# Three bf16 parts in place of one 32-bit matmul where a graph layer's sums are placed

## The chip, the cores and the metric

The kernel runs on one core of one Trainium2 chip. The metric is the device time of one launch in microseconds (us); the median of three runs of the kernel before is 1866.47 us (1866.22 to 1868.46).

## The reference

One layer of a graph network on 12,500 nodes with 256 channels and 200,000 edges sorted by their target:

```
h    = relu(layernorm(x))                       # 12500 x 256
agg  = segment_sum(h[src], dst, 12500)          # 200000 gathered rows, added by target
z    = (1 + eps) * h + agg
t    = relu(batchnorm(z @ W1 + b1, g1, bt1))    # 256 -> 512, statistics over all nodes
out  = relu(batchnorm(t @ W2 + b2 + h, g2, bt2))
x + out
```

All inputs and outputs are 32-bit floats.

## The kernel before

The kernel has three stages: tables are made ready, then the edges are summed and `z @ W1` is made (up to about 1,670 us of the span), then the second half of the layer follows. The change lies in the middle stage, so only this one is told.

**Groups and steps.** The 1,563 tiles of 128 edges are cut into 131 groups of 12 tiles (`NG`, `GT`). One loop goes over the groups; its pass i is called step i here. Groups 0 to 29 (`LEAD`) are the lead-in: their rows are gathered from `x` and normalised on the way. From group 30 on the rows come from `h_two`, a table in DRAM that holds h times 2048 (`GAIN`) as two 16-bit halves, high and low.

**A regular group** goes through these functions, each in a step of its own, so that several groups are under way at once:

- `gather(i)`: 12 indirect DMAs of 128 rows, issued by POOL (line 649), four regular groups ahead of their use, into one of four buffers.
- `edges(i)`: DVE writes the 0/1 matrix that says which edge belongs to which of 128 target positions (line 712).
- `sums(i)`: PE multiplies it with the gathered rows, 24 16-bit matmuls of 128x256 behind the lead-in (line 753). The sum of a group is 128 positions by 256 channels, in 32-bit floats, in half a bank of PSUM. Behind the lead-in one bank (`ps`) serves all groups: even and odd ones take its two halves in turn.
- `hold(i-1)`, in step i: the finished sum is copied from PSUM to a tile `zs` in SBUF (line 814, DVE behind the lead-in, ACT in it).
- `spots(i-2)`: DVE writes `at`, 128x256, which has one entry per position, at the column where that position lies in a window of 256 nodes. Behind the lead-in the entry is 1/2048 (line 826).
- `put(i-3)`: "placing". For each half of the channels one matmul with `zs` as weights and `at` as moving operand turns the sum and shifts it to its columns; the result is 128 channels by 256 nodes (line 838). A 32-bit matmul stands in the profile as two records, so a put is four.
- `add(i-4)`: DVE adds the placed sum to `zc`, the chunk of 512 nodes that it belongs to (line 856).

When all groups of a chunk are added, `slice_of` multiplies the chunk with a quarter of W1 (line 868, four records), and ACT copies the result out.

**Counted groups.** 22 groups are not gathered. They come in 11 pairs (`COUNTED`: 41 and 42, 50 and 51, up to 122 and 123, then 124 and 125). For a pair the kernel counts how often each node stands among its sources (`count`, line 1073, from marks that DVE writes in lines 1051 and 1058) and multiplies the counts with the whole of `h_two`, read by SP in pieces (`weigh`, line 1091). This work is spread as small units between the matmuls of the regular steps. Its sum is 128x512 for each group of the pair, the high and the low part side by side. `hold_pair` (line 816) adds the two with a `reduce_sum` (line 808) into a place that stays in SBUF, at the step behind the last unit of the pair; that place then goes through `put` as any other. In the steps of the two counted groups themselves PE has only a slice and a put.

**What sets the order.** Each engine works off its own queue in the order in which the program was written; a table (`plan`, `marking`) says which unit falls into which step. In a step behind the lead-in DVE has, in this order: the statistics of the last slice, `add(i-4)`, `edges(i+2)`, `spots(i-2)`, `hold_pair`, `hold(i-1)`, then the marks of this step. PE has, in this order: a slice where one is due, the first two matmuls of `sums(i)`, and then the units and the other matmuls of the group in turn, with `put(i-3)` at about two thirds. The last groups (126 to 130) are handled by `place`, which writes `hold`, `put` and `add` of the same group one right behind the other; groups 129 and 130 go without hold and put.

Of the kernel before, what the change touches and what calls it, by code (L numbers as in the profile page):

```python
# [8 lines left out]
F32 = mybir.dt.float32  # L9
# [9 lines left out]
P = 128  # L19
# [5 lines left out]
LEAD = 30  # L25
# [23 lines left out]
def kernel(  # L49
# [16 lines left out]
    nc = tc.nc  # L66
    N, D = x.shape
# [49 lines left out]
    def move(eng, sb, table, g, store):  # L117
# [33 lines left out]
    lands = [  # L151
        (consts.tile([P, LOW, D], F32, name=f"gta{k}"), consts.tile([P, GT - LOW, D], F32, name=f"gtb{k}"))
        for k in range(EARLY)
    ]
# [29 lines left out]
    at = 0  # L184
# [6 lines left out]
    with ExitStack() as es:  # L191
# [20 lines left out]
        at = 0  # L212
# [9 lines left out]
        with tc.issue_after(placed.ins):  # L222
# [36 lines left out]
            pb, lhsT=first, rhs=dstT[:, : NG * GT].rearrange("p (g t) -> p g t", t=GT)[:, :, 0],  # L259
            start=True, stop=True,  # L260
# [5 lines left out]
        for i in range(EARLY):  # L266
            for t in reversed(range(GT)):
                k = i * GT + t
# [50 lines left out]
        both = raw.tile([1, 12], F32, name="both")  # L319
# [90 lines left out]
    def fast():  # L410

        parts = []
        for n0, w in chunks:
            n = w * R
# [20 lines left out]
        with ExitStack() as fs:  # L435
# [15 lines left out]
            with ExitStack() as es:  # L451
                rows_pool = es.enter_context(tc.tile_pool(name="rows", bufs=RING))
                side_pool = es.enter_context(tc.tile_pool(name="side", bufs=1))
                sel = es.enter_context(tc.tile_pool(name="sel", bufs=2))
# [32 lines left out]
                col, start = near_pe[:, : BLOCKS * WD], near_pe[:, CH - NG :]  # L487
# [185 lines left out]
                def span(i):  # L673
                    return STEP * i - MARGIN, STEP * i - MARGIN + WIDE

                def width(i):
                    return min(WIDE, N - span(i)[0])
# [15 lines left out]
                zc, ohs, summed, zss, ats, placed, slices = {}, {}, {}, {}, {}, {}, {}  # L693
# [110 lines left out]
                def hold(i):  # L804
                    if i in COUNTED:
                        r = COUNTED.index(i) % 2
                        both, zss[i] = totals[r], kept_totals[r]
                        nc.vector.reduce_sum(
                            zss[i], both.rearrange("p (s d) -> p d s", s=2), axis=mybir.AxisListType.X
                        )  # L810
                        return
                    zss[i] = sel.tile([P, D], F32, name="zs", bufs=5)
                    copy = nc.vector.tensor_copy if i >= LEAD else nc.scalar.copy
                    copy(zss[i], summed.pop(i))  # L814

                def hold_pair(i):

                    for j in range(PAIRS_):
                        if i == ended[j] + 1:
                            for k in COUNTED[2 * j : 2 * j + 2]:  # L820
                                hold(k)

                def spots(i):
                    ats[i] = sel.tile([P, WIDE], F32, name="at", bufs=3)
                    n = width(i)
                    nc.vector.tensor_scalar(
                        ats[i][:, :n], col[:, :n], shift[:, i : i + 1], 1.0 if i < LEAD else 1.0 / GAIN,
                        op0=OP.is_equal, op1=OP.mult,
                    )

                def put(i):

                    zs, at = zss.pop(i), ats.pop(i)
                    turn_ = max(i - (NG - CLOSE - 4), 0) % 2
                    pz = own[turn_] if own else ps_z.tile([P, DC, WIDE], F32, name="pz2")
                    n = width(i)
                    for d in range(DC):
                        nc.tensor.matmul(  # L838
                            pz[:, d, :n], lhsT=zs[:, d * P : (d + 1) * P], rhs=at[:, :n], start=True, stop=True
                        )  # L840
                    placed[i] = pz

                def add(i):
# [64 lines left out]
                def half_of(v):  # L908
                    return v.bitcast(BF16)

                def halves_of(tile_, *sizes):

                    v, at, got = tile_.rearrange("p c d -> p (c d)"), 0, []
                    for n in sizes:
                        got.append(v[:, at : at + n // 2])
                        at += n // 2
                    return got

                parts_of, BMARK = [], 0
# [7 lines left out]
                    [v.bitcast(F16).rearrange("p (a m) -> p a m", m=P) for v in of_r[:2]] for of_r in places_  # L927
                ]
                b_places = [of_r[2] for of_r in places_] + halves_of(more[3], *[BMARK] * 7)
                *of_land, total_0, total_1 = halves_of(lands[1][0], *[BMARK] * 4, 2 * D, 2 * D)  # L930
                kept_totals = total_0, total_1
                b_places += halves_of(lands[0][0], *[BMARK] * 4) + of_land
                last_rows, last_a, *more_b = halves_of(spare, ROWS, AMARK, *[BMARK] * 3)
                b_marks = [half_of(v) for v in b_places + more_b]
                a_marks = [
# [9 lines left out]
                totals, keys = [], {}  # L945
# [29 lines left out]
                for j in range(PAIRS_):  # L975
                    until = -(-len(steps) * (j + 1) // PAIRS_)
                    part, done = steps[done:until], until
                    units = [unit for s in range(j * NQ, (j + 1) * NQ) for unit in phase(s)]
                    total, spent = sum(map(price, units)), 0.0
# [8 lines left out]
                for i in sorted(plan):  # L988
                    for kind, s, n in plan[i]:
                        if kind == "count":  # L990
                            j, r = s // NQ, n // WINDOWS
# [109 lines left out]
                def first(c):  # L1101

                    return min(i for i in range(NG) if c in reach(i))
# [18 lines left out]
                for c in range(NCH):  # L1122
                    k = min(max(first(c) - 2, c + 2), NG - CLOSE - 1)
# [4 lines left out]
                for i in range(NG - CLOSE):  # L1128
# [23 lines left out]
                    if i >= 2:  # L1152
                        spots(i - 2)
                    hold_pair(i)
                    while kept <= (i - 2 if kept < LEAD else i - 1):
                        if kept not in COUNTED:
                            hold(kept)
                        kept += 1
# [20 lines left out]
                    def puts():  # L1179
                        if i >= 3:  # L1180
                            put(i - 3)
# [26 lines left out]
                DIRECT, PAIR = NG - 2, (FINAL, FINAL + 1)  # L1208
                assert added == kept - 3 == FINAL - 2 and PAIR == (NG - CLOSE - 2, NG - CLOSE - 1)
                put(FINAL - 1)  # L1210
                spots(NG - CLOSE)
                added_set = set(range(added))
                for c in range(2):
# [3 lines left out]
                def place(k):  # L1217
                    if k < DIRECT:
                        hold(k)
                        put(k)  # L1220
                    place_rest(k)
# [9 lines left out]
                for i in range(NG - CLOSE, NG + 1):  # L1231
# [4 lines left out]
                    if i + 1 < DIRECT:  # L1236
                        spots(i + 1)
# [59 lines left out]
            both = tin.tile([P, 2, CH], F32, name="third")  # L1297
# [27 lines left out]
            with tc.tile_pool(name="ps_y", bufs=2, space=PSUM, reuse_waits="tile") as ps_y:  # L1325
# [165 lines left out]
                p = PAIRS - 1  # L1491
# [309 lines left out]
    with tc.If(off == 0):  # L1801
        fast()
# [32 lines left out]
```

## Time and profile before

| what | value |
|---|---|
| median of three runs | 1866.47 us |
| the profiled execution | 1868.74 us, its span 1866.9 us |
| PE busy | 1604.2 us, 86% of the span |
| DVE busy | 1121.6 us, 60% |
| ACT busy | 827.8 us, 44% |
| POOL busy | 1318.4 us, 71% |
| granted TensorE clock, mean | 0.94 |
| records of line 838 | 428 from `zs`, 88 from kept places: 129 puts of four |
| holds by DVE (line 814) | 77, 423 ns each |

The profile gives for each group of instructions its busy time, the mean of one, and the idle time of the engine just before it with what ended it. The chain of waits is followed back from the last instruction. In the timeline a row is the start, the duration (of all instructions of the row), the engine, the line, the operation, how many, and in brackets the idle time before the first and what ended it. Idle gaps of POOL that say "issue" are time in which POOL waited for nothing that the profile shows.

### The profile page before, as it was taken

The page shows a single profiled execution, that of the slowest core. Times are in us where ns is not written, and L with a number is a line of the kernel's source. Part 1 is how long each engine was busy: PE and PEld are TensorE (multiplying, and loading weights), DVE is VectorE, ACT ScalarE, POOL GpSimd, SP SyncE. Part 2 cuts the span into 40 slices and gives each one's busy share as a digit, 9 for nine tenths or more (in the row PEclk, how much of TensorE's full clock was granted, in tenths as well). Part 3 has the DMA queues.
Part 4 walks back from the last instruction along what each step waited for, and adds up shares of the span by engine and source line. Part 5 has one row for each costly group of instructions (what it writes and reads, how often), then busy time and mean ns, then how long its engine had stood idle before and what let it go on. Part 6 is the DMA issues. An engine that isn't in the chain of part 4 may idle for free.

```text
span 1866.9 us, 22422 instructions
## 1 busy us (share of the span) xinstructions
PE 1604.2 (86%) x7812; PEld 991.4 (53%) x7812; DVE 1121.6 (60%) x1723; ACT 827.8 (44%) x1537; POOL 1318.4 (71%) x1345
## 2 busy tenths in 40 slices
PE   3565676777689999999999999999999999989996
PEld 2454454555455555555555555555555555554445
DVE  6666666674854564646465364756455473448997
ACT  3776676776233333333333333333333333325546
POOL 7777777777777777777777777777777777715640
PEclk9777887888799999999999999999999999999999
DMA  6576676766467887888888788887888888859898
GB/s 199 174 223 215 211 222 211 218 201 195 138 195 246 257 256 242 267 270 253 255 262 265 240 256 270 257 251 246 273 259 263 268 250 277 239 176 324 307 337 320
DMA packets 173063, 456.66 MB, mean 245 GB/s; under 512 B 30883, under 2 KB 58699, under 8 KB 172941
## 3 DMA queue, kind: packets, MB, share of 16 engines
q1 hardware_dynamic: 95657, 258.63, 41.4%
q0 software_dynamic: 62336, 170.28, 31.8%
q10 hardware_dynamic: 14948, 26.23, 3.9%
q8 instruction: 63, 1.03, 0.2%
q14 instruction: 59, 0.48, 0.1%
HBM read 390.97 MB, written 64.05 MB: 244 GB/s over the span
## 4 chain that ended last, share of the span: by engine, by line
PE 57%; DVE 12%; DMA 10%; POOL 10%; issue 6%; ACT 4%; SPq 0%; ACTq 0%; POOLq 0%; DVEq 0%
PE ph L1091 11%; PE ps L1091 10%; PE ps L753 9%; POOL gt L649 8%; PE ph L1073 6%; PE ph L868 5%; DVE stg L520 4%; PE pz L838 4%; PE pz L1073 3%; DMA gta<-in_x_dram,srcT 3%; PE one L1374 3%; DMA gt<-in_x_dram,srcT 2%; PE pr L1374 2%; PE pq L1374 2%; DMA more<-in_x_dram,srcT 2%
## 5 line engine op out<-in xcount | busy, mean ns | idle before, releaser
L649 POOL DMA_INDIRECT gt<-h_two,srcT x939 | 889.9, 948 | 286.3 <-issue 277.2
L753 PE MATMUL ps<-gt,oh 128*128 128x256 f16 (+1 forms) x2136 | 425.1, 296 | 26.7 <-DVE zs L814 23.6
L1078 ACT CAST more<-ph 128x420 f16<-128x420 f32 (+1 forms) x437 | 224.6, 517 | 367.3 <-PE ph L1073 363.4
L856 DVE TENSOR_TENSOR zc<-pz,zc 128x512 f32<-128x512 f32 (+7 forms) x185 | 92.0, 523 | 385.2 <-PE pz L838 385.2
L753 PEld LDWEIGHTS <-oh 128*128 128x128 f16 x1848 | 182.7, 99 | 217.0 <-issue 50.0
L1091 PE MATMUL ph<-gtb,more 128*128 128x512 f16 x720 | 274.3, 381 | 1.2 <-DMA gtb<-h_two 1.2
L1091 PE MATMUL ps<-gtb,more 128*128 128x512 f16 x720 | 272.7, 379 | 0.0
L1091 PEld LDWEIGHTS <-more 128*128 128x128 f16 x2156 | 212.4, 99 | 111.6 <-issue 2.8
L868 PE MATMUL ph<-zc,w1s 128*128 128x512 f32 (+1 forms) x304 | 166.0, 675 | 69.3 <-ACT ts L886 33.4
L1078 ACT CAST more<-pz 128x420 f16<-128x420 f32 (+1 forms) x223 | 115.4, 517 | 165.3 <-PE pz L1073 161.3
L712 DVE TENSOR_TENSOR oh<-col,dstT 128x1536 f16<-128x1536 f32 (+1 forms) x107 | 187.2, 1750 | 0.0
L649 POOL DMA_INDIRECT gt<-in_x_dram,srcT x144 | 140.3, 974 | 43.9 <-issue 18.9
L1051 DVE TENSOR_TENSOR more<-col,keys 128x1536 bf16<-128x1536 f32 x88 | 152.1, 1751 | 0.8
L838 PE MATMUL pz<-at,zs 128*128 128x256 f32 x428 | 120.6, 407 | 28.5 <-DVE zc L856 22.8
L1073 PEld LDWEIGHTS <-more 128*128 128x128 bf16 x1056 | 103.4, 98 | 65.8
L1091 PE MATMUL ph<-oh,more 128*128 128x512 f16 x358 | 136.1, 380 | 0.7 <-DMA oh<-h_two 0.7
L1091 PE MATMUL ps<-oh,more 128*128 128x512 f16 x358 | 135.5, 378 | 0.0
L886 ACT COPY ts<-ph 128x512 f32<-128x512 f32 x74 | 43.4, 586 | 190.8 <-PE ph L868 163.2
L868 PEld LDWEIGHTS ph<-zc,w1s 128*128 128x128 f32 x304 | 60.1, 214 | 119.6 <-issue 58.4
L838 PEld LDWEIGHTS pz<-at,zs 128*128 128x128 f32 x428 | 82.1, 206 | 51.8 <-DVE zc L856 29.9
L649 POOL DMA_INDIRECT gta<-in_x_dram,srcT x80 | 80.8, 1010 | 24.4 <-issue 11.3
L814 DVE COPY zs<-ps 128x256 f32<-128x256 f32 x77 | 32.6, 423 | 107.1 <-PE ps L753 107.1
(265 smaller groups left out, 2487.5 us busy)
## 6 DMA issues: line engine op xcount, KB each, us to landing
gtb<-h_two SPq DMA_DIRECT2D x176, 512.0 KB
oh<-h_two SPq DMA_DIRECT2D x88, 512.0 KB
t_tab<-ts ACTq DMA_DIRECT2D x96, 256.0 KB
gt<-h_two,srcT POOLq DMA_INDIRECT x939, 4.1
h_two<-more SPq DMA_DIRECT2D x24, 512.0 KB
h_cols<-gt SPq DMA_DIRECT2D x24, 512.0 KB
zc<-h_cols SPq DMA_DIRECT2D x24, 512.0 KB
yT<-h_cols SPq DMA_DIRECT2D x24, 512.0 KB
```

What stands on the lines that cost most here:

```text
L520: reader = nc.vector.bn_stats(st[:, c : c + 2, :].rearrange("p c s -> p (c s)"), two.rearrange("p c d -> p d c"),)
L649: fetch = nc.gpsimd.indirect_dma_start(out=slot(ga, t - t0)[:rows], out_offset=None, in_=x if i < LEAD else h_two, in_offset=bass.Indirect ...
L712: nc.vector.tensor_tensor(oh, col[:, :P].unsqueeze(1).to_broadcast([P, n, P]), dstT[:, t0 : t0 + n].unsqueeze(2).to_broadcast([P, n, P]), ...
L753: part = nc.tensor.matmul(ps, lhsT=lhsT, rhs=side, start=(j == order[0] and side is sides[0]), stop=(j == order[-1] and side is sides[-1]),)
L838: nc.tensor.matmul(pz[:, d, :n], lhsT=zs[:, d * P : (d + 1) * P], rhs=at[:, :n], start=True, stop=True)
L856: nc.vector.tensor_add(side, pz[:, :, a - lo : b - lo], side)
L868: nc.tensor.matmul(ph[:, :n], lhsT=w1s[:, d, f * P : (f + 1) * P], rhs=zc[c][:, d, :n], start=(d == 0), stop=(d == DC - 1),)
L1051: nc.vector.tensor_tensor(a_marks[n % len(a_marks)], col[:, :P].unsqueeze(1).to_broadcast([P, GT, P]), keys[r][:, q, :].unsqueeze(2).to_br ...
L1073: nc.tensor.matmul(ph[:, :wide].rearrange("p (a d) -> p a d", d=WD)[:, :, lo:hi], lhsT=a_mark[:, w * WT + t, :], rhs=b_mark[:, at : at + b ...
L1078: nc.scalar.copy(counts[r][s % 2][:, : blocks(q), w * WD : (w + 1) * WD], ph[:, :wide].rearrange("p (a d) -> p a d", d=WD),)
L1091: nc.tensor.matmul(totals[r], lhsT=counts[r][s % 2][:, a % BLOCKS, :], rhs=rows[:, at, :], start=(a == 0), stop=(a == NB - 1),)
L1374: nc.tensor.matmul(ps, lhsT=w[:, k, :], rhs=t[:, k, :], start=(k == 0), stop=(k == DC - 1))
```

## The change

Behind the lead-in `hold` makes three bf16 parts of the 32-bit sum, and `put` takes three 16-bit matmuls for each half of the channels, added up in PSUM:

- ACT rounds the sum to bf16 (part 0). DVE subtracts part 0 from the sum, in place, rounds the remainder (part 1) and subtracts that again, which leaves part 2. For a regular group the sum is worked on where it lies, in its half of the PSUM bank; for a counted one `reduce_sum` now writes a small tile `zc` in SBUF, of which there is one, and the parts go to the kept place, which grows from 512 to 768 16-bit numbers.
- `at` is written as bf16 behind the lead-in; 1/2048 is exact in it.
- the tile `zs` is half as long again, and there are three of it, not five.

In the lead-in the sum is copied by ACT as before, and placed by one 32-bit matmul a half.

```diff
                 def hold(i):
                     if i in COUNTED:
                         r = COUNTED.index(i) % 2
-                        both, zss[i] = totals[r], kept_totals[r]
-                        nc.vector.reduce_sum(
-                            zss[i], both.rearrange("p (s d) -> p d s", s=2), axis=mybir.AxisListType.X
-                        )
+                        zss[i], both = kept_totals[r], totals[r]
+                        z = sel.tile([P, D], F32, name="zc", bufs=1)
+                        nc.vector.reduce_sum(z, both.rearrange("p (s d) -> p d s", s=2), axis=mybir.AxisListType.X)
+                    else:
+                        zss[i], z = sel.tile([P, 3 * D // 2], F32, name="zs", bufs=3), summed.pop(i)
+                    if i < LEAD:
+                        nc.scalar.copy(zss[i][:, :D], z)
                         return
-                    zss[i] = sel.tile([P, D], F32, name="zs", bufs=5)
-                    copy = nc.vector.tensor_copy if i >= LEAD else nc.scalar.copy
-                    copy(zss[i], summed.pop(i))
+                    zss[i] = of_three(zss[i])
+                    nc.scalar.copy(zss[i][:, 0, :], z)
+                    nc.vector.tensor_sub(z, z, zss[i][:, 0, :])
+                    nc.vector.tensor_copy(zss[i][:, 1, :], z)
+                    nc.vector.tensor_sub(zss[i][:, 2, :], z, zss[i][:, 1, :])
+
+                def of_three(v):
+                    return half_of(v).rearrange("p (k d) -> p k d", k=3)
...
                     ats[i] = sel.tile([P, WIDE], F32, name="at", bufs=3)
+                    if i >= LEAD:
+                        ats[i] = half_of(ats[i])
...
+                    parts_ = [zs] if i < LEAD else [zs[:, k, :] for k in range(3)]
                     for d in range(DC):
-                        nc.tensor.matmul(
-                            pz[:, d, :n], lhsT=zs[:, d * P : (d + 1) * P], rhs=at[:, :n], start=True, stop=True
-                        )
+                        for part in parts_:
+                            nc.tensor.matmul(
+                                pz[:, d, :n], lhsT=part[:, d * P : (d + 1) * P], rhs=at[:, :n],
+                                start=part is parts_[0], stop=part is parts_[-1],
+                            )
                     placed[i] = pz
...
-                *of_land, total_0, total_1 = halves_of(lands[1][0], *[BMARK] * 4, 2 * D, 2 * D)
-                kept_totals = total_0, total_1
-                b_places += halves_of(lands[0][0], *[BMARK] * 4) + of_land
+                kept_totals = []
+                for k in range(2):
+                    *of_land, total = halves_of(lands[k][0], *[BMARK] * 4, 3 * D)
+                    b_places += of_land
+                    kept_totals.append(total)
```

`half_of` reads a 32-bit tile as twice as many bf16 numbers. Lines behind the change move: line 838 of before is 850 of the change, 856 is 869, 868 is 881, 1051 and 1058 are 1066 and 1073, 1073 and 1091 are 1088 and 1106.

Three places show how the instructions stand. First DVE's queue at a step with `hold_pair` (here the seventh pair), from the add to the marks. Before:

```order
L856 TENSOR_TENSOR zc<-pz_3136,zc 128x2x256 [waits DVE_49,PE_49]
L712 TENSOR_TENSOR oh<-col,dstT 128x1536
L826 TENSOR_SCALAR at<-col,shift 128x256
L808 TENSOR_REDUCE gta_80<-ph 128x256 [waits PE_49]
L808 TENSOR_REDUCE gta_80<-ps 128x256 [waits PE_49]
L814 COPY zs<-ps 128x256 [waits PE_49]
L1051 TENSOR_TENSOR more_347<-col,keys 128x1536 x2
```

And of the change (`gta_78` and `gta_80` are where the kept sums of the pair lie, `zc` with 256 columns is the small tile, `ps` the bank of the regular sums):

```order
L836 TENSOR_SCALAR at<-col,shift 128x256
L809 TENSOR_REDUCE zc<-ph 128x256 [waits PE_49]
L817 TENSOR_TENSOR zc<-zc,gta_78 128x256 [waits Activation_49]
L818 CAST gta_78<-zc 128x256 [waits DVE_49]
L819 TENSOR_TENSOR gta_78<-zc,gta_78 128x256 [waits DVE_49]
L809 TENSOR_REDUCE zc<-ps 128x256 [waits DVE_49,PE_49]
L817 TENSOR_TENSOR zc<-zc,gta_80 128x256 [waits Activation_49]
L818 CAST gta_80<-zc 128x256 [waits DVE_49]
L819 TENSOR_TENSOR gta_80<-zc,gta_80 128x256 [waits DVE_49]
L817 TENSOR_TENSOR ps<-ps,zs 128x256 [waits Activation_49]
L818 CAST zs<-ps 128x256 [waits DVE_49]
L819 TENSOR_TENSOR zs<-ps,zs 128x256 [waits DVE_49]
```

Where three instructions stood, eleven stand, all ahead of the marks, and three of them wait for ACT. ACT's queue at the same step, of the change (the last counts of the step before stand ahead, the copy of the slice behind):

```order
L1093 CAST more_346<-ph 128x20x21 [waits PE_49]
L816 CAST gta_78<-zc 128x256 [waits DVE_49]
L816 CAST gta_80<-zc 128x256 [waits DVE_49]
L816 CAST zs<-ps 128x256 [waits PE_49]
L899 COPY ts<-ph 128x512 [waits PE_49]
```

Before, ACT had nothing between these two. PE's queue at the same step, where a slice stands ahead of the first matmul of the group. Before:

```order
L868 MATMUL ph<-zc,w1s 128x512 [waits whole5,Activation_49]
L868 MATMUL ph<-zc,w1s 128x512
L753 LDWEIGHTS oh
L753 MATMUL ps<-gt,oh 128x256 [waits DVE_49]
L753 LDWEIGHTS oh
L753 MATMUL ps<-gt,oh 128x256
```

And of the change:

```order
L881 MATMUL ph<-zc,w1s 128x512 [waits whole5,Activation_49]
L881 MATMUL ph<-zc,w1s 128x512
L753 LDWEIGHTS oh
L753 MATMUL ps<-gt,oh 128x256 [waits DVE_49]
L753 LDWEIGHTS oh
L753 MATMUL ps<-gt,oh 128x256
```

The first matmul of a group waits for DVE in both: before for the copy in line 814 of the group ahead, in the change for line 819 of the group ahead, the last of its hold. A put is one row `L838 MATMUL pz_3136<-at,zs 128x256 x2` before, and six pairs of LDWEIGHTS and MATMUL in line 850 in the change.

## The prediction

> **What bounds the kernel now.** I read the page, the waits, the timeline of single steps, the groups by form, and the windows for the clock. The waits first (who waited for whom: us, times, longest):
>
> ```profile
> POOL gt L649 <- issue: 296.1, 971, 0.3
> PE ps L753 <- DVE zs L814: 23.6, 16, 7.8
> PE pz L838 <- DVE zc L856: 22.8, 11, 7.9
> PE ph L868 <- DMA gt<-h_two,srcT: 15.0, 10, 3.0
> ```
>
> No gap of POOL is longer than 0.3 us: the gathers run at their own pace and never wait for a buffer. PE waits ten times for gathered rows, 15.0 us in all. So PE and the gathers are nearly even: whatever makes PE faster is soon lost in waits for rows, and whatever makes PE slower lasts, once those few us are eaten. The gathers end early enough to leave the end to PE:
>
> ```profile
> 1640.64 0.94 POOL L649 DMA_INDIRECT gt<-h_two,srcT  x1 [0.30 <-issue]
> 1653.52 0.78 PEld L798 LDWEIGHTS <-gt 128*128 128x128 f16 x8
> ```
>
> The last gather is issued at 1640.64; PE begins with group 129, the last full one, at 1653.52. The end of this stage is PE's, and in its last steps DVE's. What PE waits for at the start of a step shows here, without a slice and with one:
>
> ```profile
> 1153.39 0.38 PE L753 MATMUL ps<-gt,oh 128*128 128x256 f16 x2
> 1154.29 0.60 PE L753 MATMUL ps<-gt,oh 128*128 128x256 f16 x4 [0.51 <-DVE zs L814]
> ...
> 1165.97 0.38 PE L753 MATMUL ps<-gt,oh 128*128 128x256 f16 x2
> 1166.19 1.88 PE L868 MATMUL ph<-zc,w1s 128*128 128x512 f32 x4
> 1167.91 0.60 PE L753 MATMUL ps<-gt,oh 128*128 128x256 f16 x4
> ```
>
> Without a slice PE's next group starts 0.90 us after the last two matmuls of the one before, held by DVE's hold, although it writes the other half of the bank. With a slice the start is 1.94 us later, and a hold of 0.42 us is hidden. [...]
>
> **What the change saves.** A put and the 16-bit matmuls of the same width, near the end:
>
> ```profile
> 1648.52 1.47 PE L753 MATMUL ps<-gt,oh 128*128 128x256 f16 x12
> 1649.83 1.03 PE L838 MATMUL pz<-at,gta 128*128 128x256 f32 x4
> 1650.70 0.49 PE L753 MATMUL ps<-gt,oh 128*128 128x256 f16 x3
> ```
>
> Twelve take 1.31 us, 0.109 each; a put takes 0.87. Six 16-bit ones are 0.65, so a put saves 0.21 us. 99 puts lie behind the lead-in, 21 us in all.
>
> **What it adds to the hold.** The prices, by form:
>
> ```profile
> L814 DVE COPY zs<-ps 128x256 f32<-128x256 f32 x77 | 32.6, 423 | 107.1 <-PE ps L753 107.1
> L814 ACT COPY zs<-ps 128x256 f32<-128x256 f32 x30 | 11.2, 372 | 33.8 <-PE ps L753 32.6 <-ACT ts L886 1.2
> L856 DVE TENSOR_TENSOR zc<-pz,zc 128x256 f32<-128x256 f32 x16 | 6.0, 417 | 17.5 <-PE pz L838 17.5
> L808 DVE TENSOR_REDUCE gta<-ph 128x256 f32<-128x512 f32 x11 | 7.6, 691 | 18.1 <-PE ph L1091 18.1
> L886 ACT COPY ts<-ph 128x512 f32<-128x512 f32 x74 | 43.4, 586 | 190.8 <-PE ph L868 163.2
> L588 ACT ACTIVATE more<-more 128x1024 f16<-128x1024 f32 x16 | 16.9, 1058 | 0.5
> ```
>
> ```profile
> 1651.51 0.15 DVE L767 TENSOR_TENSOR off<-shift,row 128x1 f32<-128x1 f32 x1
> 1651.69 0.23 DVE L769 TENSOR_SCALAR to<-dstT,off 128x3 f32<-128x3 f32 x1
> ```
>
> Before, one copy of 0.42. Now ACT 0.37, then three instructions of DVE of 0.42, each of which needs the one before; L769, which reads what L767 wrote, started 0.03 behind its end. 0.37 + 0.03 + 3 x 0.45 make 1.75; of the last 0.45 only the instruction's own 0.42 counts, which leaves 1.72. Against the 0.42 of before that is 1.30; Handing on from engine to engine may take a little longer than from DVE to itself, so I take 1.36. Whether ACT's rounding or DVE's writing into PSUM costs more, no row shows: the bounds are 1.05 (the three overlapping, 0.34 apart, as independent copies do) and 1.70 (0.1 more for each). What it does to PE, place by place:
>
> 1. *Steps without a slice*: PE waits for all of it, +1.36. From group 43 to 121 there are 63 regular steps; leaving out the first of each run of seven and the steps with a pair, I count 14 of this kind in the timeline: 19 us.
>
> 2. *Steps with a slice*: the hold now ends 0.90 + 1.36 = 2.26 after the last matmuls, the slice at 1.94: +0.32, in 31 steps: 10 us.
>
> 3. *Steps with hold_pair.* The seventh pair:
>
> ```profile
> 1239.73 0.69 DVE L808 TENSOR_REDUCE gta<-ph 128x256 f32<-128x512 f32 x1 [0.88 <-PE ph L1091]
> 1240.94 0.41 DVE L814 COPY zs<-ps 128x256 f32<-128x256 f32 x1
> 1241.69 0.38 PE L753 MATMUL ps<-gt,oh 128*128 128x256 f16 x2
> ```
>
> The hold that PE waits for stands behind the pair's in DVE's queue. Before, it was through at 1241.35, in time. Now each of the two is 0.69 for the reduce, 0.42 for ACT from SBUF (1058 ns for 1024 columns, less 768 columns at 0.83 ns, the slope from 372 ns for 256 columns to 586 for 512), 0.03 behind both, and three times 0.45: 2.5; two are 5.0, and the group's own three are 1.35. PE starts 6.4 us behind the first reduce, not 1.96: +4.4 us (3.4 to 5.5), ten times before the end: 44 us. Nothing covers it: PE's units of this step stand behind the waiting matmul.
>
> 4. *Steps of counted groups.* There PE's second put waits for the add ahead, and that add stands in DVE's queue behind hold and marks:
>
> ```profile
> 1072.82 0.42 DVE L814 COPY zs<-ps 128x256 f32<-128x256 f32 x1 [1.41 <-PE ps L753]
> 1077.10 0.74 DVE L856 TENSOR_TENSOR zc<-pz,zc 128x256 f32<-128x256 f32 x2
> 1077.90 2.05 PE L838 MATMUL pz<-at,zs 128*128 128x256 f32 x4 [2.53 <-DVE zc L856]
> ```
>
> I find such a wait, 2.53 here, at nine of the ten places, so +1.36 each: 12 us. At the tenth (from 1597) DVE itself waits for the slice, and hides it.
>
> 5. *The tail.* Here hold, put and add of a group follow one another:
>
> ```profile
> 1644.02 1.10 PE L838 MATMUL pz<-at,zs 128*128 128x256 f32 x4 [0.61 <-DVE zs L814]
> 1647.56 1.13 PE L838 MATMUL pz<-at,gta 128*128 128x256 f32 x4 [1.78 <-DVE at L826]
> 1652.76 1.13 PE L838 MATMUL pz<-at,zs 128*128 128x256 f32 x4 [1.24 <-DVE zs L814]
> ```
>
> Groups 126 and 127 +1.36 each, the pair +3.6, group 128 +0.9 (ACT is done early): 7 us.
>
> Sum: 19 + 10 + 44 + 12 + 7 = 92. Off go the puts that lie on the path, some 80 of the 99 (those whose end waits for DVE anyway and those before group 40 do not count): 17. Off go also the waits for rows from group 40 on, about 10 of the 15.0. That leaves +62 us.
>
> **The clock.** In rows of 3.4 us (engines' busy us, then PEclk):
>
> ```profile
> 1040.40:1043.80 3.40, 3.40 (x4) 1.25 (x5) 1.66 (x1) 0.00 (x0) 2.49 (x4) 0.50 0.59 211
> 1282.80:1286.20 3.40, 1.27 (x5) 0.84 (x5) 3.40 (x7) 0.59 (x1) 2.57 (x3) 1.00 0.73 198
> 1286.20:1289.60 3.40, 3.40 (x5) 1.19 (x5) 3.40 (x8) 0.00 (x0) 2.71 (x3) 0.50 0.40 121
> 1392.00:1395.40 3.40, 1.58 (x6) 1.24 (x7) 3.40 (x7) 1.15 (x1) 2.49 (x4) 1.00 0.85 254
> 1395.40:1398.80 3.40, 3.40 (x18) 1.77 (x18) 3.37 (x8) 1.30 (x3) 2.62 (x3) 1.00 0.49 122
> ```
>
> After a stretch in which PE was busy 1.27 of 3.40 us the clock was 0.50 for the next; after 1.58 it stayed at 1.00. So idling over about 2 us within one stretch costs up to 1.7 us. The ten waits of 4.4 us must each do this; a part of the half-speed stretch is still idle, so I take 1.4: 14 us. The nine of point 4 grow by 1.36, this one to 3.9, and do it more often than before: net 4. The drop at 1040 comes from waits for rows; that it goes, I count -2. Net +16. [...]
>
> The sum is 62 + 16 = +78 us, made against the profiled execution's 1868.74 (span 1866.9 and 1.8 around it), which lies 2.3 over the median of the runs. For the median: 1866.5 + 78 = 1944 us.
>
> **The rivals.**
>
> [...]
> - *A longer chain*: 0.1 us more for each instruction (1.70 and 5.5) gives 14 x 1.7 + 31 x 0.66 + 55 + 9 x 1.7 + 9 - 27 = 96, and drops on nearly all waits, 25: 1987 us. No row shows DVE writing back into the bank it reads.
> - *The rows decide*, and DVE's chain is hidden: if the first matmul of a group were not held by the bank, only points 4 and 5 would stay, and less than the waits for rows takes up; a few us in the tail remain, 1869 us. Against it stands 0.51 in the row of 1154.29.
> - *Faster*: all 21 us of the puts come through, 1846 us. It needs the hold to be hidden behind the slice, so a chain less than 1.04 us longer (1.94 less 0.90), and gathers that end sooner; POOL has only its 0.3 us gaps to give. It decides only if PE were the sole bound and DVE never asked.
>
> That three 16-bit matmuls are no cheaper than one of 32 bits is excluded by 0.65 against 0.87.
>
> **How the numbers follow.** The main case has 0.50, no more drops 0.24, the longer chain 0.17, rows decide 0.05, faster 0.04. The likeliest gives 1944. With the short bounds (1.05 and 3.4, no drops) the sum is 14 x 1.05 + 34 + 9 x 1.05 + 5 - 27 = 36, 1902; the long one gives 1987. For 8 in 10 I take nearly all of that, 1905 to 1985. A measurement here can tell about 0.2%, 3.7 us, from no change: faster 0.04, same 0.04 (most of the rows' case), slower 0.92.
>
> **What would show it.** In the profile of the changed kernel: line 753 idle for DVE's line 819, not 23.6 but some 75 us, with ten waits over 4 us; six records of line 850 in 0.65 us; lines 817 to 819 near 420 ns each; POOL with gaps over 0.3 us that PE's line 753 ends; more stretches at half clock. Wrong would be the prediction if those ten waits were absent, or if PE still waited for rows in the second half.

## The result, and the profile after

The changed kernel takes 1968.89 us (median of six runs), the kernel before 1865.67 us beside it: 1.056 times as long, interval 1.0545 to 1.0575. It is 103 us slower; one of the six took 5718 us, a slow run that the ratio and its interval leave out. The forecast was slower by 78, 1944 us in a range of 1905 to 1985: the sign and the range held, and the size was 25 us short. The profiled execution of the change has a span of 1966.2 us, 99.3 more than that of before; the rest of this text divides these 99.3.

The waits of the change (who waited for whom: us, times, longest), where before line 753 waited 23.6 us for DVE and POOL never lost more than 0.3 us at a time:

```profile
POOL gt L649 <- PE ps L753: 94.0, 48, 13.7
PE ps L753 <- DVE zs L819: 92.6, 43, 8.7
PE pz L850 <- DVE zc L869: 38.4, 12, 7.7
PE ph L881 <- DMA gt<-h_two,srcT: 7.8, 4, 2.7
```

PE waits for DVE's last instruction of a hold, and now POOL waits for PE: a gather finds its buffer still in use for 94 us in all. PE's waits for gathered rows at the slice fell from 15.0 to 7.8 us. The gathers, which were even with PE, are now held back by it.

The groups by form give the new instructions (busy us, mean ns):

```profile
L817 DVE TENSOR_TENSOR ps<-ps,zs 128x256 f32<-128x256 f32 x77 | 33.2, 431 | 138.3 <-ACT zs L816 138.3
L818 DVE CAST zs<-ps 128x256 bf16<-128x256 f32 x77 | 32.7, 424 | 2.7
L819 DVE TENSOR_TENSOR zs<-ps,zs 128x256 bf16<-128x256 f32 x77 | 32.6, 424 | 2.6
L816 ACT CAST zs<-ps 128x256 bf16<-128x256 f32 x77 | 28.7, 373 | 45.4 <-PE ps L753 43.5
L818 DVE CAST gta<-zc 128x256 bf16<-128x256 f32 x22 | 6.9, 312 | 0.8
```

Each of DVE's three instructions takes what the one copy took, as priced; writing back into PSUM costs next to nothing (431 against 424 ns), and ACT's rounding takes what its copy took (373 against 372). The one price that is off is the rounding of a counted sum out of SBUF, 312 ns and not 420.

A start without a slice and one with a slice, of the change:

```profile
1190.64 0.38 PE L753 MATMUL ps<-gt,oh 128*128 128x256 f16 x2
1192.87 0.60 PE L753 MATMUL ps<-gt,oh 128*128 128x256 f16 x4 [1.84 <-DVE zs L819]
...
1204.34 0.38 PE L753 MATMUL ps<-gt,oh 128*128 128x256 f16 x2
1204.56 1.88 PE L881 MATMUL ph<-zc,w1s 128*128 128x512 f32 x4
1206.57 0.60 PE L753 MATMUL ps<-gt,oh 128*128 128x256 f16 x4
```

Between the starts of the last matmuls of one group and the first of the next lie 2.23 us in both cases, against 0.90 and 1.94 before: +1.33 and +0.29 (forecast +1.36 and +0.32). Now the step with the seventh hold_pair, DVE first and then PE:

```profile
1282.53 0.69 DVE L809 TENSOR_REDUCE zc<-ph 128x256 f32<-128x512 f32 x1 [0.88 <-PE ph L1106]
1283.69 0.42 DVE L817 TENSOR_TENSOR zc<-zc,gta 128x256 f32<-128x256 f32 x1 [0.47 <-ACT gta L816]
...
1285.04 0.69 DVE L809 TENSOR_REDUCE zc<-ps 128x256 f32<-128x512 f32 x1
1286.21 0.43 DVE L817 TENSOR_TENSOR zc<-zc,gta 128x256 f32<-128x256 f32 x1 [0.47 <-ACT gta L816]
...
1287.36 0.42 DVE L817 TENSOR_TENSOR ps<-ps,zs 128x256 f32<-128x256 f32 x1
1288.28 0.42 DVE L819 TENSOR_TENSOR zs<-ps,zs 128x256 bf16<-128x256 f32 x1
```

```profile
1282.76 1.88 PE L881 MATMUL ph<-zc,w1s 128*128 128x512 f32 x4
1288.76 0.59 PE L753 MATMUL ps<-gt,oh 128*128 128x256 f16 x2 [4.12 <-DVE zs L819]
1289.71 0.64 PE L753 MATMUL ps<-gt,oh 128*128 128x256 f16 x2
```

PE starts 6.2 us behind the first reduce (forecast 6.4, before 1.96). The rows behind the wait show a second part of the price: two matmuls take 0.59 to 0.64 us where they take 0.38 elsewhere. The windows give the clock (the seventh column after the time range):

```profile
1283.70:1287.10 3.40, 0.94 (x3) 0.21 (x2) 2.69 (x7) 1.17 (x3) 2.49 (x4) 0.99 0.95 377
1287.10:1290.50 3.40, 1.74 (x8) 1.02 (x8) 3.33 (x6) 0.51 (x1) 2.48 (x4) 0.50 0.71 193
```

From the starts of all groups in both traces the 99.3 us divide so:

| where | forecast | measured |
|---|---|---|
| steps without a slice (13 places) | 19 | 15.4 |
| steps with a slice (32) | 10 | 9.9 |
| steps with hold_pair (10) | 44 | 37.3 |
| boundaries at counted groups (9) | 12 | 16.7 |
| waits for rows that vanish | -10 | within the rows above |
| shorter puts and slower clock, within the groups 39 to 120 | -17 + 16 | +9.2 |
| tail, from the start of group 121 to the end of the stage | 7 | 7.9 |
| rest: up to group 39 -1.8, last stage +4.7 | 0 | +2.9 |
| sum | 81 | 99.3 |

The first four rows are the growth of the time between the last matmul of a group and the first of the next. Of the rest, the part up to the start of group 30 (-4.3) and the last stage (+4.7) are not touched by the change. Over the eight undisturbed traces here the last stage lies between 202.6 and 207.3 us; before has the shortest and the change the longest, so I take that difference for chance. Groups 30 to 38 cost 2.5.

### The profile page after: what moved, and what is told of

Its sections match the earlier page's. It is cut to its first block, busy times and chain, and to the rows that moved or that the text cites. A ratio compares the mean times of both kernels' runs of the same rounds, so it can differ in the third digit from the quotient of the medians.

```text
span 1966.2 us, 23146 instructions
## 1 busy us (share of the span) xinstructions
PE 1614.6 (82%) x8010; PEld 984.3 (50%) x8010; DVE 1209.0 (61%) x1943; ACT 860.9 (44%) x1636; POOL 1319.0 (67%) x1345
## 4 chain that ended last, share of the span: by engine, by line
PE 52%; DVE 18%; DMA 10%; POOL 6%; ACT 6%; issue 5%; SPq 0%; ACTq 0%; DVEq 0%; POOLq 0%
PE ph L1106 11%; PE ps L1106 10%; PE ps L753 9%; PE ph L1088 6%; POOL gt L649 5%; DVE stg L520 4%; PE pz L1088 3%; PE pz L850 3%; DMA gta<-in_x_dram,srcT 3%; PE one L1389 3%; PE ph L881 2%; DMA gt<-in_x_dram,srcT 2%; PE pr L1389 2%; PE pq L1389 2%; DMA more<-in_x_dram,srcT 2%
## 5 line engine op out<-in xcount | busy, mean ns | idle before, releaser
L753 PE MATMUL ps<-gt,oh 128*128 128x256 f16 (+1 forms) x2136 | 433.2, 300 | 94.6 <-DVE zs L819 92.6
L1106 PE MATMUL ph<-gtb,more 128*128 128x512 f16 x720 | 279.9, 389 | 1.1 <-DMA gtb<-h_two 1.1
L1106 PE MATMUL ps<-gtb,more 128*128 128x512 f16 x720 | 277.6, 386 | 0.0
L850 PE MATMUL pz<-at,zs 128*128 128x256 bf16 (+1 forms) x582 | 105.3, 316 | 45.1 <-DVE zc L869 37.8
L817 DVE TENSOR_TENSOR ps<-ps,zs 128x256 f32<-128x256 f32 x77 | 33.2, 431 | 138.3 <-ACT zs L816 138.3
L1410 POOL TENSOR_TENSOR ax<-ax,by 128x1024 f32<-128x1024 f32 x10 | 27.3, 2726 | 85.6 <-ACT by L1367 81.7
```

What stands on the lines that cost most here:

```text
L753: part = nc.tensor.matmul(ps, lhsT=lhsT, rhs=side, start=(j == order[0] and side is sides[0]), stop=(j == order[-1] and side is sides[-1]),)
L850: nc.tensor.matmul(pz[:, d, :n], lhsT=part[:, d * P : (d + 1) * P], rhs=at[:, :n], start=part is parts_[0], stop=part is parts_[-1],)
L1106: nc.tensor.matmul(totals[r], lhsT=counts[r][s % 2][:, a % BLOCKS, :], rhs=rows[:, at, :], start=(a == 0), stop=(a == NB - 1),)
```

## The experiments

Two sets of runs (those labelled below as the first and second disturbed set) were taken while everything ran slowly: the kernel before itself took 2379 and 2336 us there, and the chip of the first set gave 1865 in another. What slowed it stays open, since these traces lack two thirds of the records that tell of a DMA's landing. POOL was held up in them as it is not before (its longest wait before is 0.3 us), here in the kernel with the puts alone:

```profile
POOL gt L649 <- PE ps L753: 417.8, 69, 21.3
```

In such a set the place of a wait can't be priced, so the argument rests on the runs of other sets.

**The chain alone: only regular groups are split.** Counted groups are summed straight into the kept place as before, and placed by one 32-bit matmul a half.

```diff
                     if i in COUNTED:
                         r = COUNTED.index(i) % 2
-                        zss[i], both = kept_totals[r], totals[r]
-                        z = sel.tile([P, D], F32, name="zc", bufs=1)
-                        nc.vector.reduce_sum(z, both.rearrange("p (s d) -> p d s", s=2), axis=mybir.AxisListType.X)
-                    else:
-                        zss[i], z = sel.tile([P, 3 * D // 2], F32, name="zs", bufs=3), summed.pop(i)
+                        zss[i] = kept_totals[r][:, :D]
+                        nc.vector.reduce_sum(
+                            zss[i], totals[r].rearrange("p (s d) -> p d s", s=2), axis=mybir.AxisListType.X
+                        )
+                        return
+                    zss[i], z = sel.tile([P, 3 * D // 2], F32, name="zs", bufs=3), summed.pop(i)
...
-                    if i >= LEAD:
+                    if i >= LEAD and i not in COUNTED:
                         ats[i] = half_of(ats[i])
...
-                    parts_ = [zs] if i < LEAD else [zs[:, k, :] for k in range(3)]
+                    parts_ = [zs] if i < LEAD or i in COUNTED else [zs[:, k, :] for k in range(3)]
```

> Once more, only regular groups are split in three parts, in PSUM as in the change; counted ones are held and placed as before. My theory: the waits of about 6 us in the steps with hold_pair fall to 2.1 to 2.3, some 36 us in ten steps, with them the half-speed stretches behind them (18 us, as the filled waits showed), and 4 us in the tail, against 4 more for 32-bit puts: about 1915 us (1905 to 1925). Rival, the pair matters little and the chain of every step makes the loss: 1950 or more.

Measured: 1915.1 us, 1.0267 times before (1.0249 to 1.0284), 54 less than the change. The same step, PE:

```profile
1260.66 0.38 PE L753 MATMUL ps<-gt,oh 128*128 128x256 f16 x2
1260.88 1.88 PE L882 MATMUL ph<-zc,w1s 128*128 128x512 f32 x4
1263.25 0.38 PE L753 MATMUL ps<-gt,oh 128*128 128x256 f16 x2 [0.48 <-DVE zs L820]
```

The start is 2.59 us behind the last matmuls, not 6.2. From group 43 on, the nine groups that follow such a wait are 18.7 us shorter together than in the change, and the gaps at their ends are the same. So about half of the loss belongs to the counted pairs (54 us) and half to the regular chain (50). The same kernel in the first and second disturbed set:

> Only regular groups are split in three parts, counted ones are held and placed as before. My theory: the waits of about 6 us in the ten steps with hold_pair fall to 2.1 to 2.3, some 38 us, with them the half-speed stretches behind them, some 17, and 4 us in the tail, against 4 more for 32-bit puts: about 1912 us (1900 to 1922). Rival, the pair matters little and the chain of every step makes the loss: 1950 or more.

> Only regular groups are split in three parts, in PSUM as in the change; counted ones are held and placed as before. My theory: the waits of about 6 us in the steps with hold_pair fall to 2.1 to 2.3, some 36 us in ten steps, with them the half-speed stretches behind them (18 us, as the filled waits showed), and 4 us in the tail, against 4 more for 32-bit puts: about 1915 us (1905 to 1925). Rival, the pair matters little and the chain of every step makes the loss: 1950 or more.

There 2417.6 and 2373.0 us, 1.017 and 1.014 times before. The counterpart, only the counted groups split, was run in these two sets alone:

> Only counted groups are split in three parts, regular ones are held by one copy and placed by one 32-bit matmul a half. My theory: steps without a pair start as before (0.79 and 1.83 us behind the last matmuls), the ten with hold_pair wait about 5.1 us, 32 us more than before, the clock drops behind them cost 16 and the tail 4: about 1912 us (1900 to 1922). Rival, only the regular chain counts: 1870.

> Only counted groups are split in three parts; regular ones are held by one copy and placed by one 32-bit matmul a half. My theory: steps without a pair start as before (0.79 and 1.83 us behind the last matmuls), the ten with hold_pair wait about 5.1 us, 32 us more than before, the clock drops behind them cost 18 and the tail 4, the boundaries little: about 1918 us (1905 to 1928). Rival, only the regular chain counts: 1870.

2402.2 and 2358.4 us, 1.0097 and 1.0094 times before. Both halves cost something there too (none of the four intervals reaches down to 1.005); the sizes expected for an undisturbed chip are not tested by them.

**The order in DVE's queue.** The regular hold stands ahead of the pair's.

```diff
-                    hold_pair(i)
                     while kept <= (i - 2 if kept < LEAD else i - 1):
                         if kept not in COUNTED:
                             hold(kept)
                         kept += 1
+                    hold_pair(i)
```

> Once more, the changed kernel with hold(i-1) ahead of hold_pair in DVE's queue. My theory: the two banks of the pair stay taken for as long, so PE's wait moves from the first matmul of the group to the first weighing of the next pair, about 1.3 us behind it, and is 1 to 2 us shorter: 1955 us (1942 to 1965). Rival, the order in DVE's queue alone makes the wait: it falls to 2.3 us, and time to about 1915.

Measured: 1945.8 us, 23 less than the change, 1.0441 times before (1.0422 to 1.046). The start of the group is at 2.2 us again, and the wait moved, as expected, but not to where I put it:

```profile
1272.78 0.38 PE L753 MATMUL ps<-gt,oh 128*128 128x256 f16 x2
...
1273.51 0.46 PE L1088 MATMUL ph<-more,more 128*128 128x420 bf16 x2
1276.78 0.46 PE L1088 MATMUL ph<-more,more 128*128 128x420 bf16 x2 [2.80 <-ACT ts L899]
```

PE waits 2.8 us at the third count, for the bank that ACT frees by copying the slice out. That copy stands in ACT's queue behind the pair's two roundings, and each of those waits for DVE's reduce (in the seventh pair's step of the change ACT idles 2.59 and 2.12 us before them, until DVE's line 809 ends). So the pair's split holds PE through a third engine's queue, and the order in DVE's queue was worth 23 of the 54 us that the pair costs. In the first disturbed set the same kernel took 2422.4 us, 1.0162 times before:

> The changed kernel with hold(i-1) ahead of hold_pair in DVE's queue. My theory: the two banks of the pair stay taken for as long, so PE's wait moves from the first matmul of the group to the first weighing of the next pair, about 1.3 us behind it, and is 1 to 2 us shorter: 1955 us (1942 to 1965). Rival, the order in DVE's queue alone makes the wait: it falls to 2.3 us, and time to about 1915.

**The clock by itself.** In nine of the ten steps with hold_pair 16 idle matmuls of 512 columns go into the bank of the slice, which the slice then overwrites. The tenth, at the start of group 57, has no slice and stays as it was.

```diff
+                    if fill is not None:
+                        for _ in range(FILL):
+                            nc.tensor.matmul(
+                                ph, lhsT=last_oh[fill][:, 0, :], rhs=last_oh[fill][:, 1:5, :].rearrange("p a b -> p (a b)"),
+                                start=True, stop=True,
+                            )
                     for d in range(DC):
                         nc.tensor.matmul(
                             ph[:, :n], lhsT=w1s[:, d, f * P : (f + 1) * P],
```

> The changed kernel with 16 idle 16-bit matmuls of 512 columns (some 3.5 us) ahead of the slice in the steps with hold_pair, into the bank that the slice then overwrites. PE still waits for the hold, but it is busy while it does. My theory: the wait itself costs the same, and the clock does not drop behind it, 2 us in each of eight or nine steps: about 1951 us (1944 to 1958). Rival, the 2 us that the group behind a pair's step loses have another cause, or idling is not what lowers the clock: 1969, or more where the idle matmuls are in the way.

Measured: 1948.8 us, 20 less than the change, 1.0454 times before (1.042 to 1.0488). The same step (lines are two higher):

```profile
1276.22 0.38 PE L755 MATMUL ps<-gt,oh 128*128 128x256 f16 x2
1276.44 3.62 PE L884 MATMUL ph<-oh 128*128 128x512 f16 x16
1279.89 1.88 PE L889 MATMUL ph<-zc,w1s 128*128 128x512 f32 x4
1282.38 0.38 PE L755 MATMUL ps<-gt,oh 128*128 128x256 f16 x2 [0.60 <-DVE zs L821]
```

The group starts as late as in the change, 6.2 us behind the last matmuls, but PE idles 0.60 us and not 4.12, and its first matmuls take 0.38 us. From group 43 on, eight waits are filled. The groups behind them are 16.9 us shorter than in the change, 1.7 to 2.7 each, with the same gaps at their ends, and none of the eight waits is followed by half speed any more. At group 57, without a fill, PE waits 5.84 us and the clock drops as in the change. More work on PE made the kernel faster: such a wait costs its length and, through the clock, about 2 us more.

**The bank freed at once.** Every sum leaves PSUM with one instruction (a copy, or the reduce) into a 32-bit tile, and the split works on that, behind all copies of the step. DVE has one instruction more for each regular group than in the change. There is one such tile for the regular groups and one for each of a pair; a pool of three tiles for all groups would leave 4.84 KB per partition of SBUF for another pool of 6 KB.

```diff
+                        z = sel.tile([P, D], F32, name="zc", bufs=1)
+                        nc.vector.tensor_copy(z, summed.pop(i))
+                    unsplit.append((zss[i], z))
+
+                unsplit = []
+
+                def split():
+                    while unsplit:
+                        parts, z = unsplit.pop(0)
+                        nc.scalar.copy(parts[:, 0, :], z)
+                        nc.vector.tensor_sub(z, z, parts[:, 0, :])
+                        nc.vector.tensor_copy(parts[:, 1, :], z)
+                        nc.vector.tensor_sub(parts[:, 2, :], z, parts[:, 1, :])
...
                             hold(kept)
                         kept += 1
+                    split()
```

> Every sum leaves PSUM with one instruction (DVE's copy for a regular group, reduce_sum for a counted one, into 32-bit tiles in SBUF, one for each), as before the change; the split into three parts then works on that tile, behind the holds of the step and ahead of the marks. DVE does one copy more for each group than in the changed kernel. My theory (what costs is that the bank stays taken through the split): the starts of groups are as before, 0.79 and 1.83 us behind the last matmuls and about 2 in the ten steps with hold_pair, puts save 17 us, of which waits for rows take some 10 back; the adds of counted steps stay late, some 16, and the tail 8: about 1878 us (1865 to 1892). Rival, DVE's extra work itself is what costs (late marks, late adds): 1950 or more, since DVE has more to do than in the change.

Measured: 1885.4 us, 1.0116 times before (1.0098 to 1.0135), 84 less than the change. The seventh pair's step on DVE:

```profile
1239.28 0.69 DVE L813 TENSOR_REDUCE gta<-ph 128x256 f32<-128x512 f32 x1 [0.88 <-PE ph L1116]
1239.88 0.68 DVE L813 TENSOR_REDUCE gta<-ps 128x256 f32<-128x512 f32 x1
1240.48 0.42 DVE L817 COPY zc<-ps 128x256 f32<-128x256 f32 x1
1240.81 0.42 DVE L826 TENSOR_TENSOR gta<-gta 128x256 f32<-128x256 f32 x1
```

Three instructions end what PE waits for. In 34 of the 54 steps from group 44 to 121 that are no boundary, the next group now starts 0.21 us sooner than before, the price of the shorter put, to the hundredth as forecast; in most of the others one of the two traces has a wait for a DMA or a stretch at half speed. What stays are the nine boundaries, 19 us together, and the tail, since there the add, or the put, stands behind the split. It was how long the bank is held, and not DVE's load: DVE has more to do here than in the change, a copy of 0.42 us for each regular group. The run moves two things at once, the work on the bank and the order (no split stands ahead of a copy any more); the order alone was worth 23 us above.

**The split behind the add.** In the first step of a counted pair the split follows the next step's add.

```diff
                             hold(kept)
                         kept += 1
-                    split()
+                    if not (i in COUNTED and i + 1 in COUNTED):
+                        split()
...
                         added = take_and_add(added)
+                        if i in COUNTED:
+                            split()
```

> As the run in which sums are copied out of PSUM first, but in the first step of a counted pair the split stands behind the next step's add, not ahead of the marks. My theory: the nine boundaries at counted pairs, 2.1 us each over before, go back to what they were (19 us), and the rest stays: 1885 - 19 = 1866 us (1859 to 1875). Rival, the boundaries are late for another reason (DVE has 1.3 us more to do in each step): 1883.

Measured: 1885.4 us, 1.0107 times before (1.0087 to 1.0127): nothing gained, 19 us off. The mechanism worked and the time did not follow. The nine boundaries fell by 23 us; but the other steps of groups 43 to 121 grew by 16.5, with more waits for gathered rows, and the tail by 4.6:

```profile
PE ph L890 <- DMA gt<-h_two,srcT: 17.2, 7, 3.8
PE ps L753 <- DMA gt<-h_two,srcT: 7.4, 4, 3.0
```

In the run with the copy these two were 9.3 and 3.0 us. I had carried the rows as a term once and left them out here.

**The tail as before, too.** Groups from 124 on are held and placed as before the change; all others as in the last run.

```diff
+                    if i >= FINAL:
+                        if i in COUNTED:
+                            r = COUNTED.index(i) % 2
+                            zss[i] = kept_totals[r][:, :D]
+                            nc.vector.reduce_sum(
+                                zss[i], totals[r].rearrange("p (s d) -> p d s", s=2), axis=mybir.AxisListType.X
+                            )
+                            return
+                        zss[i] = sel.tile([P, 3 * D // 2], F32, name="zs", bufs=3)
+                        nc.vector.tensor_copy(zss[i][:, :D], summed.pop(i))
+                        return
...
-                    if i >= LEAD:
+                    if LEAD <= i < FINAL:
                         ats[i] = half_of(ats[i])
...
-                    parts_ = [zs] if i < LEAD else [zs[:, k, :] for k in range(3)]
+                    parts_ = [zs] if i < LEAD or i >= FINAL else [zs[:, k, :] for k in range(3)]
```

> As the run with the split behind the add, and groups from 124 on (the last pair and 126 to 128) are held and placed as before the change, by one copy and one 32-bit matmul a half. My theory: the tail, some 9 us over before in the run with the copy, comes back: 1857 us (1850 to 1865), below the kernel before, since some 80 puts are 0.21 us shorter and nothing waits for the split any more; waits for rows may take half of it. Rival, the rows decide and nothing is gained over before: 1866.

Measured: 1870.0 us, 1.003 times before (1.0019 to 1.0041). The tail came back, and the rival was nearer than my theory: nothing is gained over before. The first and the last gather from `h_two`, of before and then of this run, and this run's waits for rows:

```profile
465.67 0.95 POOL L649 DMA_INDIRECT gt<-h_two,srcT  x1 [0.30 <-ACT more L547]
1640.64 0.94 POOL L649 DMA_INDIRECT gt<-h_two,srcT  x1 [0.30 <-issue]
```

```profile
462.27 0.95 POOL L649 DMA_INDIRECT gt<-h_two,srcT  x1 [0.30 <-ACT more L547]
1642.70 0.95 POOL L649 DMA_INDIRECT gt<-h_two,srcT  x1 [0.30 <-issue]
```

```profile
PE ph L901 <- DMA gt<-h_two,srcT: 22.4, 10, 4.1
PE ps L753 <- DMA gt<-h_two,srcT: 5.9, 4, 2.7
```

The 939 gathers start 3.4 us sooner and end 2.1 later than before. However much sooner PE is ready, it waits for rows: 22.4 us at the slice against 15.0 before, and 5.9 at line 753 against 3.1. That is how I read where the gain of the shorter puts went; no run has faster gathers, so it is not shown by an experiment. Why a gather takes 1.258 us on average here and 1.253 before is open.

**The puts alone** were tried only in the first disturbed set.

```diff
-                    nc.scalar.copy(zss[i][:, 0, :], z)
-                    nc.vector.tensor_sub(z, z, zss[i][:, 0, :])
-                    nc.vector.tensor_copy(zss[i][:, 1, :], z)
-                    nc.vector.tensor_sub(zss[i][:, 2, :], z, zss[i][:, 1, :])
+                    nc.vector.tensor_copy(zss[i][:, 0, :], summed.pop(i))
...
-                    parts_ = [zs] if i < LEAD else [zs[:, k, :] for k in range(3)]
+                    parts_ = [zs] if i < LEAD or i in COUNTED else [zs[:, 0, :] for k in range(3)]
```

> The placing alone is changed: a regular sum is copied once by DVE, as bf16, and that one part is placed three times (so parts 1 and 2 are left out, and the result is not the reference's); counted groups stay wholly as before. My theory: a put of six records 0.65 us against 0.87, 77 puts, 16 us of PE's time off, some of it lost in waits for rows: 1855 us (1850 to 1862). Rival, the new form of put is itself no cheaper where it stands: 1866.

2389.1 us, 1.0045 times before (1.0018 to 1.0072): no gain, which rows that decide would give too, but no test of 1855 us on an undisturbed chip.

## Why the prediction was right, and where it was short

**What bounds the kernel** held. PE and the gathers were even, so PE's losses lasted: POOL's gaps went from 0.3 us to waits of up to 13.7. And PE's gains are lost: the versions with the later split wait for rows instead. The 15.0 us were not all that PE waited for rows before; one more wait of 3.1 us, at line 753, was left out.

**The put** saves 0.21 us, as the steps of the run with the copy show. Its six records take 0.65 us in the change, where four took 0.87:

```profile
1199.98 0.82 PE L850 MATMUL pz<-at,zs 128*128 128x256 bf16 x6
1200.63 0.38 PE L1106 MATMUL ph<-oh,more 128*128 128x512 f16 x1
```

**The bank** was the mechanism. The claim rested on the first matmul's wait, 0.51 us for the hold of the other half; with the bank freed by one instruction, and no split ahead of it, 84 of the 103 us go, while DVE does more. What the runs show is that the program makes PE wait for the bank's last reader; what the chip would do without that wait, no run here shows.

**Points 1 to 3** hold in their prices: 1.33 for 1.36, 0.29 for 0.32, 6.2 for 6.4. Of the 1.36, the 0.06 for handing on from engine to engine were my estimate, and no run shows them: in the change DVE's line 817 starts 0.03 us behind the end of ACT's rounding where it waits for it, and lines 818 and 819 start 0.03 behind DVE's own line ahead. All ten waits over 4 us came, 4.05 to 5.77 us. The pair steps sum to 37 and not 44, mainly as three of the ten started late before already (by 6 us together), which their new wait then covered, and a little as the rounding out of SBUF takes 312 ns.

**The clock** is the term that was mis-sized, 16 us in the forecast. Between 690 and 1760 us the clock drops 17 times in the change and 5 times before; with the 2 us a drop that the filled waits measured, 12 more are some 24 us, and the tenth pair's wait, at 635 us, adds one. Two steps of it failed: I took 1.4 us for a drop, and I gave the boundaries only 4. Six of the nine drop the clock now, two before. In the boundary's slice this shows at once, 3.31 us for what takes 1.88:

```profile
1225.25 1.12 PE L850 MATMUL pz<-at,zs 128*128 128x256 bf16 x6 [2.73 <-DVE zc L869]
1226.17 3.31 PE L881 MATMUL ph<-zc,w1s 128*128 128x512 f32 x4
```

That is also why point 4 came out at 16.7 and not 12: the three boundaries that drop it in neither trace grew by 1.0 to 1.2 us, the two that drop it in both by 0.7 and 0.9, and the four that drop it only now by 2.7 to 3.3. The trigger was right: the waits of more than 4 us each did it, and the run that filled them took it back.

**A slip of sums**: 92 - 17 - 10 is 65 and not 62; by its own terms the forecast was +81, 1947 us.

**The rest** of the 25 us: the median moved 103.2 and the profiled executions 99.3, of which 2.9 lie before group 39 and in the last stage, where the forecast has nothing.

Of the rivals, "no more drops", which the low bound of 1902 us took too, is shown by no run: 17 drops against 5 and the filled waits refute it. "A longer chain" is refuted by 424 to 431 ns. "The rows decide" does not hold for the change; for the versions without its waits the traces speak for it. "Faster" asked for gathers with room to spare; the last run has none.

## What to carry to other kernels

Ask of a longer sequence of instructions on a buffer not only how long it takes but how long it keeps what it reads: one copy out and the same work on the copy cost 84 us less here, though it was more work. Price a wait of the engine that bounds with the clock that it loses behind it, 1.7 to 2.7 us for each filled wait here. And when two resources are even, a saving on one may be worth nothing until the other is faster too, as in the last version here; so ask first how much sooner the other could be.

## What the runs showed of the hardware

The clock goes by stretches of 3.41 us on a fixed grid: in the traces of before and of the change all half-speed stretches start a multiple of 3.413 us apart, to 0.01 us. Counted over eight traces, from 690 us on: of the stretches at full speed, all that had PE busy for less than 1.38 of the 3.41 us were followed by one at half speed, and of those with more only six were (two of 1.38, then 1.40, 1.46, 1.55 and 1.77 us). Two neighbours, of the change and of the run with the hold first (time range, length, PE's busy time; PEclk is the third number from the end):

```profile
1396.30:1399.70 3.40, 1.31 (x4) 0.34 (x3) 2.37 (x6) 1.33 (x4) 2.79 (x3) 1.00 0.92 346
1399.70:1403.10 3.40, 1.28 (x6) 0.82 (x6) 3.30 (x6) 1.27 (x3) 2.49 (x4) 0.50 0.77 227
```

```profile
951.30:954.70 3.40, 1.41 (x9) 0.81 (x9) 2.76 (x6) 1.95 (x5) 2.49 (x4) 1.00 0.51 175
954.70:958.10 3.40, 3.40 (x22) 1.95 (x21) 3.23 (x3) 1.27 (x3) 2.50 (x3) 1.00 0.74 163
```

PE idled 2.09 us in the first stretch of the one pair and 1.99 in that of the other: behind the one came half speed, behind the other not. So of two waits of about 2 us, one may cost nothing and the other about 2 us more, as the filled waits have it. I had expected DVE's in-place writes into PSUM to cost up to 0.1 us; they cost 7 ns (431 against 424). And a rounding copy out of SBUF takes 312 ns where the same out of PSUM takes 424 (line 818 of the change, 22 and 77 of them); why, no run here shows.
